# A graph-attention kernel whose adjacency mask is stored in another fp8 format and turned into its second form on another engine

## Chip, cores and metric

The kernel runs on one core of one Trainium2 chip. The metric is the device time in microseconds (us) of one execution. Where the text speaks of the profile, it is one profiled execution on that core: PE is the matrix engine (TensorE), PEld its weight loads, DVE the vector engine (VectorE), ACT the activation engine (ScalarE), POOL the general engine (GpSimd), SP the queue that issues most DMAs.

## What is computed

Two layers of masked multi-head attention over 16 images of 1024 nodes with 256 features, each behind a layer norm and a ReLU, with a residual. The layers differ in the number of heads (4 and 8), in the biases, and in the test on the adjacency: layer 0 keeps an edge where it is above 0, layer 1 where it is not 0.

```python
# layer 0
h = jnp.maximum(_layernorm(x, axis=-1), 0.0)
Q, K, V = ...                        # 4 heads of 64
scores = jnp.einsum('bhne,bhme->bhnm', Q, K) * scale
mask = adjacency_matrices[:, None, :, :] > 0
scores = jnp.where(mask, scores, -jnp.inf)
attn = jax.nn.softmax(scores, axis=-1)
x = x + heads(attn @ V) @ Wo.T + bo
# layer 1
h = jnp.maximum(_layernorm(x, axis=-1), 0.0)
q, k, v = ...                        # 8 heads of 32, with biases
scores = jnp.einsum('bhnd,bhmd->bhnm', q, k) / math.sqrt(D)
mask = adjacency[:, None, :, :] == 0
scores = jnp.where(mask, -jnp.inf, scores)
w = jax.nn.softmax(scores, axis=-1)
x = x + heads(w @ v) @ Wo.T + bo
```

The adjacency of the inputs holds zeros and ones. The kernel computes for any 32-bit integers: a fast program runs first, without subtracting the maximum of the scores; if a sum of exponentials left the range from 1e-15 to 1e15, a second, careful program does everything again (`verdict` and the `tc.If` at the end decide; it doesn't run with these inputs).

## The kernel before

**Stages and steps.** The fast program is one stream of steps. A stage is one layer of one image; the order is layer 0 of image 0, then for each image b layer 0 of image b+1 followed by layer 1 of image b, and at the end layer 1 of image 15. A layer-0 stage has 16 steps, a layer-1 stage 32. A step works on four blocks of 128 keys by 512 queries. `scores` (L400) makes them in two PSUM pairs, in layer 1 with four heads side by side in 32 rows of the array, in layer 0 with two in 64 rows. `exponentials` takes each pair through one VectorE instruction (L416: mask times BIG, minimum with the score, so that a masked score becomes hugely negative) and one exponential on ScalarE (L421). `weigh` (L433) multiplies by the values two steps later (LEAD = 2). The sums of exponentials come from additions of tiles, on VectorE and GpSimd in layer 0 (`add_tiles`, L442 to L448), on GpSimd (L534) and by accumulating DMAs (L520) in layer 1, and then from a matmul with a column block of ones (`count`, L301), are copied out (L320), spread by DMA (L333) and inverted (L341).

**Work around the stream.** Everything else is put by hand at numbered steps with `later(i, f, ...)` and is issued in step i after its exponentials. In one step, what has a place in `LARGE` or is a `turn` comes last (`rank`), so a `second` always comes ahead of a `turn`, `k`, `q`, `values` or `end_half` of the same step; otherwise the order is that of registration. An even step with such a large piece puts off its `weigh` to the next step. The pieces: `stats` and `norm` of the next inputs (L173, L174, GpSimd's L177 to L183, L190 on ScalarE), `turn` (transposes L208, copied by L209 on ScalarE), `k` and `q` (L225, copied by L231 to L239), `values` (L262, copied by L266), `end_half` (L381, added by L386). All of these and the scores share one PSUM pool of three pairs (`ps_s`, bufs=3), handed out in program order. A group's output (L433) is copied out of PSUM by L312 on ScalarE, between the two exponentials of a step, before the next group may weigh.

**The mask.** GpSimd issues the load of a tile of the adjacency as bf16 (L128), SP a DMA transpose (L134), and `put` (L143, ScalarE) writes adjacency - 0.5 in fp8 (float8e4) into one of five buffers of 8 x 512 bytes per partition. With BIG = 1e20 that is what layer 0 needs: above 0 is positive, all else negative. After layer 0 of the image has used it, `second` (L151, VectorE) rewrites two key blocks of a buffer at a time in place, to +0.5 where the adjacency is not 0 and -0.5 where it is. There are eight `second` per image. For images 0 to 14 they stand in the first 14 steps of layer 0 of the next image (steps a, a+2, a+4, a+6, a+8, a+10, a+12, a+13 with a that stage's first step). Image 15 has no next image: its eight stand in layer 1 of image 14, at steps c+8, c+10, ... c+22 with c that stage's first step.

**The test of the sums.** `test` (L247, VectorE) compares the spread sums of one layer of one image with the two bounds and multiplies the result into `chk`, 32 columns at a time: two instructions in layer 0 (32 columns of sums), four in layer 1 (64 columns). `chk` has 32 columns; `verdict` takes its minimum over columns (L742) and adds over partitions by a matmul (L744).

Of the kernel before, what the change touches and what calls it, by code (L numbers as in the profile page):

```python
# [10 lines left out]
F32 = mybir.dt.float32  # L11
BF16 = mybir.dt.bfloat16
I32 = mybir.dt.int32
F8 = mybir.dt.float8e4
AF = mybir.ActivationFunctionType
ALU = mybir.AluOpType
PSUM = bass.MemoryType.PSUM

P = 128
# [8 lines left out]

SUM_MIN, SUM_MAX = 1e-15, 1e15

BIG = 1e20

# [8 lines left out]
def load_weights(nc, const, a):  # L43

    w, loads = Weights(), []

    def mat(src, name):
        t = const.tile([P, 2, 256], F32, tag=name, name=name)
        loads.append((t, src.rearrange("(c p) f -> p c f", p=P)))
        return t  # L50

    def row(src, name):
        t = const.tile([P, 256], F32, tag=name, name=name)
        loads.append((t, src.partition_broadcast(P)))
        return t

    def col(src, name):
        t = const.tile([P, 2], F32, tag=name, name=name)
        loads.append((t, src.rearrange("(c p) -> p c", p=P)))
        return t  # L60

    w.k, w.q, w.v, w.o = [], [], [], []

    def mats(layer):
        for kind, of in (("k", w.k), ("q", w.q), ("v", w.v), ("o", w.o)):
            of.append(mat(a[f"w{kind}{layer}"], f"w{kind}{layer}"))

    mats(0)
    w.bo = [row(a["bo0"], "bo0"), row(a["bo1"], "bo1")]
    w.bq = col(a["bq1"], "bq1")  # L70
    w.bk = col(a["bk1"], "bk1")
    w.bv = col(a["bv1"], "bv1")
    mats(1)
    w.ident = const.tile([P, P], F32, tag="ident", name="ident")
    make_identity(nc, w.ident)
    w.ones = const.tile([P, 64], F32, tag="ones", name="ones")
    nc.gpsimd.memset(w.ones, 1.0)
    w.mhalf = const.tile([P, 4], F32, tag="mhalf", name="mhalf")
    nc.gpsimd.memset(w.mhalf, -0.5)
    return w, loads  # L80


def fast_program(ctx, tc, a, w, loads, chk):
# [3 lines left out]
    nc = tc.nc  # L87
    x, adj, out = a["x"], a["adj"], a["out"]
# [30 lines left out]
    class Mask:  # L119
# [16 lines left out]
        def put(self, t):  # L136

            qh = t // 4
            if t % 4 == 0:
                self.m[qh] = actp.tile(  # L140
                    [P, NT, 512], F8, tag="mask", bufs=5, name=f"mask_{self.b}_{qh}"
                )
            nc.scalar.activation(  # L143
                self.m[qh][:, :, ts(t % 4, P)], self.flipped.pop(t), AF.Identity,
                bias=w.mhalf[:, 0:1], saturate=False,
            )

        def second(self, u):

            m = self.m[u // 4][:, ts(u % 4, 2), :]  # L150
            nc.vector.tensor_scalar(  # L151
                m, m, -0.5, 0.5, op0=ALU.not_equal, op1=ALU.subtract, saturate=False
            )


    class Inputs:
# [85 lines left out]

        def test(self):

            for k in range(self.sums.shape[1] // 32):
                for bound, op in ((SUM_MIN, ALU.is_ge), (SUM_MAX, ALU.is_le)):
                    nc.vector.scalar_tensor_tensor(  # L247
                        out=chk, in0=self.sums[:, ts(k, 32)], scalar=bound, in1=chk,
                        op0=op, op1=ALU.mult,
                    )  # L250

        def k(self, half):
            self.kq(half, False)
# [18 lines left out]
    class Group:  # L272
# [23 lines left out]
        def count(self, p, start, stop):  # L296

            if start:
                self.s = ps_o.tile([P, 512], F32, tag="pz", name=f"pz_{self.n}")
            for r in range(self.per):  # L300
                nc.tensor.matmul(  # L301
                    self.s[r * self.D : (r + 1) * self.D, :], w.ones[:, : self.D], p[:, r, :],
                    start=start, stop=stop,
                )

# [11 lines left out]
        def spread(self):  # L317

            s = work.tile([P, 512], F32, tag="s", bufs=1, name=f"s_{self.n}")
            nc.scalar.copy(s, self.s)  # L320
            inp, k = self.inp, 2 * self.qh + self.g
            if k == 0:

                pool, tag = small, f"sums{self.layer}"
                if self.layer and inp.b == B - 1:
                    pool, tag = adjp, "adj"
                inp.sums = pool.tile(
                    [P, 4 * self.n_f], F32, tag=tag, bufs=1, name=f"sums_{inp.n}"
                )
            self.sn = inp.sums[:, k * self.n_f : (k + 1) * self.n_f]  # L330
            lanes = P // self.per
            for r in range(self.per):
                nc.sync.dma_start(  # L333
                    self.sn[r * lanes : (r + 1) * lanes, :],
                    s[r * self.D : r * self.D + 1, :].rearrange("r (c f) -> r c f", f=self.n_f),
                )
# [70 lines left out]
    def exponentials(st, between):  # L407


        gr = st.gr  # L410
        odd = st.j % 2
        st.p = pp.tile([P, 4, 512], F32, tag=f"p{odd}", bufs=2 if odd else 7, name=f"p_{st.n}")
        for i in range(2):
            half = st.p[:, ts(i, 2), :]
            kt = st.blocks[2 * i][1]
            nc.vector.scalar_tensor_tensor(  # L416
                out=half,
                in0=gr.mask.m[gr.qh][:, kt, :].unsqueeze(1).to_broadcast([P, 2, 512]),
                scalar=BIG, in1=st.ps[i], op0=ALU.mult, op1=ALU.min,
            )  # L420
            nc.scalar.activation(half, half, AF.Exp, scale=gr.scale)  # L421
            if i == 0:
                for f in between:
                    f()
# [34 lines left out]
    class Stream:  # L459
# [19 lines left out]
        def run(self):  # L479
# [3 lines left out]
            for i in range(n + LEAD):  # L483
# [21 lines left out]
                if now:  # L505
                    exponentials(now, copies)
                else:
                    for f in copies:
                        f()
# [80 lines left out]
    mask, inp = masks[0], inputs[0][0]  # L590
# [91 lines left out]
    for t in range(NT):  # L682
        i = 5 + 2 * t
# [52 lines left out]
def verdict(ctx, tc, w, chk):  # L736

    nc = tc.nc
    work = ctx.enter_context(tc.tile_pool(name="vwork", bufs=1))
    ps = ctx.enter_context(tc.tile_pool(name="vps", bufs=1, space=PSUM))  # L740
    row = work.tile([P, 1], F32, tag="row", name="row")
    nc.vector.tensor_reduce(row, chk, mybir.AxisListType.X, ALU.min)  # L742
    tot = ps.tile([1, 1], F32, tag="tot", name="tot")
    nc.tensor.matmul(tot, row, w.ones[:, 0:1], start=True, stop=True)  # L744
    bad = work.tile([1, 1], I32, tag="bad", name="bad")
    nc.vector.tensor_scalar(bad, tot, -1.0, float(P), op0=ALU.mult, op1=ALU.add)
    return bad
# [142 lines left out]
@with_exitstack  # L890
def kernel(
    ctx: ExitStack,
    tc: tile.TileContext,
    x: bass.AP,
    adj: bass.AP,
    wq0: bass.AP,
    wk0: bass.AP,
    wv0: bass.AP,
    wo0: bass.AP,
    bo0: bass.AP,  # L900
    wq1: bass.AP,
    bq1: bass.AP,
    wk1: bass.AP,
    bk1: bass.AP,
    wv1: bass.AP,
    bv1: bass.AP,
    wo1: bass.AP,
    bo1: bass.AP,
    out: bass.AP,
):  # L910
    nc = tc.nc
    a = dict(
        x=x, adj=adj, wq0=wq0, wk0=wk0, wv0=wv0, wo0=wo0, bo0=bo0, wq1=wq1, bq1=bq1,
        wk1=wk1, bk1=bk1, wv1=wv1, bv1=bv1, wo1=wo1, bo1=bo1, out=out,
    )
    B = x.shape[0]
    const = ctx.enter_context(tc.tile_pool(name="const", bufs=1))
    w, loads = load_weights(nc, const, a)
    chk = const.tile([P, 32], F32, tag="chk", name="chk")
    with ExitStack() as fast, tc.manual_schedule():  # L920
        fast_program(fast, tc, a, w, loads, chk)
    bad = verdict(ctx, tc, w, chk)
    flag = nc.values_load(bad[0:1, 0:1], min_val=0, max_val=P)
    with tc.If(flag > 0):
        with ExitStack() as careful:
            careful_program(careful, tc, a, w)
# [56 lines left out]
```

## Time and profile before

| what | us |
|---|---|
| runs: 3333.37, 3335.87, 3335.38; median | 3335.38 |
| profiled execution: span from first to last instruction | 3332.6 |
| a layer-0 stage (from 539.69 to 620.27) | 80.58 |
| a layer-1 stage (from 2867.10 to 2991.30) | 124.20 |
| layer 1 of images 14 and 15, to the end (from 3071.50) | 261.10 |
| `second` (L151): busy in all, mean of 128 | 178.6, 1.395 |
| `put` (L143): busy in all with a transposed tile, mean of 124 | 140.6, 1.135 |
| `test` (L247): busy in all, mean of 96 | 62.1, 0.647 |

The time of the profiled execution is not listed apart from its span; the runs lie 0.8 to 3.3 us above that span. The mean granted clock of TensorE is 0.993 of full speed. In a line of groups the numbers after the bar are the busy time and the mean duration in ns, and after the second bar the idle time of the engine just before. In a line of stretches each engine has its busy time with the number of instructions in brackets, then come the granted clock (1.00 is full speed), the share of the DMA engines and GB/s. In a line of the timeline come start, duration, engine, source line, operation and operands, and in square brackets the idle time of the engine just before it with what ended it. A stretch is given by its ends in us from the start of the span.

### The profile page before, as it was taken

The page shows a single profiled execution, that of the slowest core. Times are in us where ns is not written, and L with a number is a line of the kernel's source. Part 1 is how long each engine was busy: PE and PEld are TensorE (multiplying, and loading weights), DVE is VectorE, ACT ScalarE, POOL GpSimd, SP SyncE. Part 2 cuts the span into 40 slices and gives each one's busy share as a digit, 9 for nine tenths or more (in the row PEclk, how much of TensorE's full clock was granted, in tenths as well). Part 3 has the DMA queues.
Part 4 walks back from the last instruction along what each step waited for, and adds up shares of the span by engine and source line. Part 5 has one row for each costly group of instructions (what it writes and reads, how often), then busy time and mean ns, then how long its engine had stood idle before and what let it go on. Part 6 is the DMA issues. An engine that isn't in the chain of part 4 may idle for free.

```text
span 3332.6 us, 44087 instructions
## 1 busy us (share of the span) xinstructions
PE 3245.0 (97%) x16766; PEld 1272.4 (38%) x16766; DVE 2557.2 (77%) x2760; ACT 2178.2 (65%) x2402; POOL 2387.3 (72%) x1272
## 2 busy tenths in 40 slices
PE   8999999999999999999999999999999999999898
PEld 3443343433433333333434333343343343333333
DVE  5777877878778787786878768787787877878867
ACT  5567576675766757567575666757667576675565
POOL 4568586786867868677686776868778586785766
PEclk9999999999999999999999999999999999999999
DMA  7338467383664846548375573855738467482431
GB/s 145 63 67 148 97 111 140 73 153 86 121 128 82 157 83 131 113 93 149 77 141 102 105 138 77 146 103 112 138 74 152 96 112 139 80 149 52 89 77 31
DMA packets 313484, 361.08 MB, mean 108 GB/s; under 512 B 190000, under 2 KB 257840, under 8 KB 290480
## 3 DMA queue, kind: packets, MB, share of 16 engines
q0 software_dynamic: 77856, 253.78, 42.1%
q1 hardware_dynamic: 235408, 104.41, 14.0%
q8 instruction: 133, 2.18, 0.3%
q14 instruction: 87, 0.71, 0.1%
HBM read 119.54 MB, written 17.56 MB: 41 GB/s over the span
## 4 chain that ended last, share of the span: by engine, by line
PE 73%; POOL 8%; DMA 7%; DVE 5%; issue 3%; ACT 3%; SPq 1%; POOLq 0%; DVEq 0%; ACTq 0%
PE ps L400 24%; PE po L433 21%; PE pq L225 11%; PE pv L262 7%; PE py L381 5%; POOL p L534 5%; DMA p<-p 4%; DVE p L416 4%; PE pz L301 3%; DMA adjT<-adj 2%; ACT p L421 1%; PE ph L208 1%; POOL p L445 1%; ACT mask L143 1%; DVE p L442 1%
## 5 line engine op out<-in xcount | busy, mean ns | idle before, releaser
L416 DVE SCALAR_TENSOR_TENSOR p<-mask,ps 128x1024 f32<-128x1024 fp8e4 x1536 | 1790.7, 1213 | 598.6 <-PE ps L400 509.9
L421 ACT ACTIVATE p<-p 128x1024 f32<-128x1024 f32 x1536 | 1616.8, 1057 | 960.6 <-DVE p L416 915.2
L534 POOL TENSOR_TENSOR p<-p,p 128x2048 f32<-128x2048 f32 x255 | 1201.7, 4714 | 181.5 <-PE po L433 162.2
L400 PE MATMUL ps<-qT,kT 32*128 32x512 f32 (+1 forms) x6144 | 1196.0, 635 | 37.4 <-DVE p L416 35.6
L433 PE MATMUL po<-p,v 128*32 128x512 f32 (+1 forms) x6144 | 994.0, 603 | 1.0 <-ACT cat L312 0.9
L400 PEld LDWEIGHTS ps<-qT,kT 32*128 32x128 f32 (+1 forms) x6144 | 382.4, 185 | 739.5 <-issue 358.6
L446 POOL TENSOR_TENSOR p<-p 128x1024 f32<-128x1024 f32 x128 | 319.7, 2497 | 273.4 <-DVE p L445 268.4
L433 PEld LDWEIGHTS po<-p,v 128*32 128x32 f32 (+1 forms) x6144 | 229.1, 118 | 691.7 <-issue 503.6
L445 POOL TENSOR_TENSOR p<-p 128x1024 f32<-128x1024 f32 x64 | 151.4, 2366 | 236.2 <-DVE p L442 151.8
L262 PE MATMUL pv<-wv,hT 128*128 128x256 f32 x1024 | 239.5, 387 | 14.6 <-ACT hT L209 14.5
L520 POOL DMA_DIRECT2D p<-p x178 | 178.8, 1005 | 98.1 <-DMA p<-p 66.1
L225 PE MATMUL pq<-hT,wk 128*128 128x512 f32 x512 | 239.6, 611 | 2.8 <-ACT hT L209 2.8
L225 PE MATMUL pq<-hT,wq 128*128 128x512 f32 x512 | 240.0, 612 | 0.1
L381 PE MATMUL py<-wo,cat 128*128 128x256 f32 x1008 | 235.8, 387 | 3.3 <-ACT hT L209 1.0
L262 PEld LDWEIGHTS pv<-wv,hT 128*128 128x128 f32 x1024 | 190.6, 191 | 88.1 <-ACT hT L209 26.8
L381 PEld LDWEIGHTS py<-wo,cat 128*128 128x128 f32 x1008 | 188.3, 191 | 74.7 <-issue 46.3
L352 POOL TENSOR_TENSOR cat<-cat,inv 128x512 f32<-128x512 f32 x127 | 178.8, 1408 | 7.5 <-DMA inv<-vd 6.3
L151 DVE TENSOR_SCALAR mask<-mask 128x1024 fp8e4<-128x1024 fp8e4 x128 | 178.6, 1395 | 0.0
L442 DVE TENSOR_TENSOR p<-p 128x1024 f32<-128x1024 f32 x128 | 161.4, 1261 | 0.0
L448 POOL TENSOR_TENSOR p<-p,p 128x1024 f32<-128x1024 f32 x64 | 152.4, 2381 | 5.0
L301 PE MATMUL pz<-p,ones 128*32 128x512 f32 (+1 forms) x888 | 148.7, 595 | 4.6 <-DMA p<-p 3.8
L225 PEld LDWEIGHTS pq<-hT,wk 128*128 128x128 f32 x512 | 93.2, 192 | 145.1 <-issue 103.5
(50 smaller groups left out, 1696.0 us busy)
## 6 DMA issues: line engine op xcount, KB each, us to landing
p<-p POOLq DMA_DIRECT2D x178, 1024.0 KB, 8.8
adj<-in_adj_dram POOLq DMA_DIRECT2D x128, 256.0 KB, 4.4
x<-bo POOLq DMA_DIRECT2D x64, 512.0 KB, 6.0
x<-in_x_dram SPq DMA_DIRECT2D x32, 512.0 KB, 4.1
inv<-vd SPq DMA_DIRECT2D x128, 128.0 KB, 2.9
inv<-vd SPq DMA_DIRECT2D x252, 64.0 KB, 2.9
out_dram<-x SPq DMA_DIRECT2D x31, 512.0 KB, 3.1
sums<-s SPq DMA_DIRECT2D x384, 2.0 KB, 3.4
```

What stands on the lines that cost most here:

```text
L225: nc.tensor.matmul(pq[:, m, :], wt[self.layer][:, c, ts(m, P)], self.hT[half][:, c, :], start=(c == 0), stop=(c == 1),)
L262: nc.tensor.matmul(pv[:, i, :], self.hT[half][:, c, ts(i, P)], w.v[self.layer][:, c, :], start=(c == 0), stop=(c == 1),)
L301: nc.tensor.matmul(self.s[r * self.D : (r + 1) * self.D, :], w.ones[:, : self.D], p[:, r, :], start=start, stop=stop,)
L381: nc.tensor.matmul(py[:, i, :], self.half.cat[:, c, ts(i, P)], w.o[self.layer][:, c, :], start=(c == 0), stop=(c == 1),)
L400: nc.tensor.matmul(st.ps[i // 2][:, i % 2, :], gr.inp.kT[r * D : (r + 1) * D, gr.g, ts(kt, P)], gr.inp.qT[gr.qh][r * D : (r + 1) * D, gr.g ...
L416: nc.vector.scalar_tensor_tensor(out=half, in0=gr.mask.m[gr.qh][:, kt, :].unsqueeze(1).to_broadcast([P, 2, 512]), scalar=BIG, in1=st.ps[i] ...
L421: nc.scalar.activation(half, half, AF.Exp, scale=gr.scale)
L433: nc.tensor.matmul(gr.o[r * D : (r + 1) * D, :], gr.inp.v[:, kt, h * D : (h + 1) * D], st.p[:, i, :], start=(kt == 0), stop=(kt == NT - 1),)
L442: nc.vector.tensor_add(a, a, b)
L445: engine.tensor_add(b, two.p[:, 0:2, :], two.p[:, 2:4, :])
L446: nc.gpsimd.tensor_add(a, a, b)
L534: nc.gpsimd.tensor_add(one, one, st.p)
```

## The change

The mask is kept in float8e5, a format with a wider exponent. `put` now writes 2 x 8192 x adjacency - 8192, that is 8192 or -8192 for the adjacency of these inputs; layer 0 still multiplies by BIG, now 1e15. `second` becomes one activation on ScalarE: the absolute value of the first form plus 8192, that is 0 where the adjacency is 0 and 16384 where it is 1. In layer 1, L416 adds -8192 to that and takes the minimum with the score, so a masked score becomes -8192, whose exponential is 0. The places of `put` and `second` in the order of steps stay as they are.

The test takes all columns of the sums at once, two instructions in either layer, and `chk` has 64 columns for it. The block of ones shrinks to one column that `count` broadcasts, and the biases of the two activations stand in one small tile with the -0.5 that the norm uses.

```diff
-F8 = mybir.dt.float8e4
+F8 = mybir.dt.float8e5
...
-BIG = 1e20
+BIG = 1e15
+EDGE = 8192.0
...
-    w.ones = const.tile([P, 64], F32, tag="ones", name="ones")
+    w.ones = const.tile([P, 1], F32, tag="ones", name="ones")
     nc.gpsimd.memset(w.ones, 1.0)
-    w.mhalf = const.tile([P, 4], F32, tag="mhalf", name="mhalf")
-    nc.gpsimd.memset(w.mhalf, -0.5)
+    numbers = const.tile([P, 6], F32, tag="numbers", name="numbers")
+    w.mhalf, w.below, w.above = numbers[:, 0:4], numbers[:, 4:5], numbers[:, 5:6]
+    for of, value in ((w.mhalf, -0.5), (w.below, -EDGE), (w.above, EDGE)):
+        nc.gpsimd.memset(of, value)
...
             nc.scalar.activation(
                 self.m[qh][:, :, ts(t % 4, P)], self.flipped.pop(t), AF.Identity,
-                bias=w.mhalf[:, 0:1], saturate=False,
+                bias=w.below, scale=2.0 * EDGE, saturate=False,
             )
...
             m = self.m[u // 4][:, ts(u % 4, 2), :]
-            nc.vector.tensor_scalar(
-                m, m, -0.5, 0.5, op0=ALU.not_equal, op1=ALU.subtract, saturate=False
-            )
+            nc.scalar.activation(m, m, AF.Abs, bias=w.above, saturate=False)
...
-            for k in range(self.sums.shape[1] // 32):
-                for bound, op in ((SUM_MIN, ALU.is_ge), (SUM_MAX, ALU.is_le)):
-                    nc.vector.scalar_tensor_tensor(
-                        out=chk, in0=self.sums[:, ts(k, 32)], scalar=bound, in1=chk,
-                        op0=op, op1=ALU.mult,
-                    )
+            part = chk[:, : self.sums.shape[1]]
+            for bound, op in ((SUM_MIN, ALU.is_ge), (SUM_MAX, ALU.is_le)):
+                nc.vector.scalar_tensor_tensor(
+                    out=part, in0=self.sums, scalar=bound, in1=part, op0=op, op1=ALU.mult,
+                )
...
-                    self.s[r * self.D : (r + 1) * self.D, :], w.ones[:, : self.D], p[:, r, :],
+                    self.s[r * self.D : (r + 1) * self.D, :], w.ones.to_broadcast([P, self.D]), p[:, r, :],
...
-            self.sn = inp.sums[:, k * self.n_f : (k + 1) * self.n_f]
+            self.sn = inp.sums[:, ts(k, self.n_f)]
...
-                scalar=BIG, in1=st.ps[i], op0=ALU.mult, op1=ALU.min,
+                scalar=-EDGE if gr.layer else BIG, in1=st.ps[i],
+                op0=ALU.add if gr.layer else ALU.mult, op1=ALU.min,
...
-    chk = const.tile([P, 32], F32, tag="chk", name="chk")
+    chk = const.tile([P, 64], F32, tag="chk", name="chk")
```

## The prediction

> **What bounds the kernel now.** I read the busy shares first, then the groups by line for the operations that the diff touches, then the busy time of each engine in stretches cut at the stage borders (a stage is one layer of one image; the border is where the score matmuls at L400 change from 64-row to 32-row form), and last the timeline where TensorE stood still.
>
> ```profile
> PE 3245.0 (97%) x16766; PEld 1272.4 (38%) x16766; DVE 2557.2 (77%) x2760; ACT 2178.2 (65%) x2402; POOL 2387.3 (72%) x1272
> ...
> L151 DVE TENSOR_SCALAR mask<-mask 128x1024 fp8e4<-128x1024 fp8e4 x128 | 178.6, 1395 | 0.0
> ```
>
> TensorE is busy for 97%, so 87 us at most are idle; VectorE's 178.6 us in L151 are not for the taking by themselves. The question is where those 128 instructions stand.
>
> ```profile
> core 0: us, PE busy (x) PEld busy (x) DVE busy (x) ACT busy (x) POOL busy (x), PEclk, DMA share, GB/s
> ...
> 539.69:620.27 80.58, 80.24 (x345) 31.24 (x344) 67.90 (x71) 43.81 (x49) 48.44 (x27) 1.00 0.45 99
> ...
> 2867.10:2991.30 124.20, 121.64 (x698) 47.89 (x696) 91.32 (x102) 92.19 (x103) 102.03 (x55) 0.99 0.69 124
> 3071.50:3332.60 261.10, 233.22 (x1444) 87.25 (x1442) 195.12 (x194) 156.66 (x167) 178.04 (x65) 0.95 0.30 64
> ...
> 539.69:620.27 80.58, 10.58 (x8) 1.00 0.45 99
> ...
> 2867.10:2991.30 124.20, 0.00 (x0) 0.99 0.69 124
> 3071.50:3332.60 261.10, 21.01 (x8) 0.95 0.30 64
> ```
>
> The first rows are all engines, the last three L151 alone. A layer-0 stage (539.69) holds 8 of the second forms, 10.6 us of VectorE, but TensorE is idle there for 80.58 - 80.24 = 0.34 us: all of L151 is hidden. A layer-1 stage (2867.10) holds none. The last stretch, layer 1 of images 14 and 15, holds 8 that take 21.0 us, and TensorE is idle for 27.9 us. That is the only place where L151 can be on the path. Here is the worst spot of it, in order of time:
>
> ```profile
> 3114.98 8.43 DVE L151 TENSOR_SCALAR mask<-mask 128x1024 fp8e4<-128x1024 fp8e4 x1
> ...
> 3116.34 1.09 PE L208 MATMUL ph<-ident,hn 128*128 128x128 f32 x8
> 3116.71 1.61 POOL L198 DMA_DIRECT2D x<-bo  x1
> 3117.55 5.29 POOL L534 TENSOR_TENSOR p<-p,p 128x2048 f32<-128x2048 f32 x1
> 3121.99 1.70 POOL L520 DMA_DIRECT2D p<-p  x1
> 3123.32 2.34 DVE L416 SCALAR_TENSOR_TENSOR p<-mask,ps 128x1024 f32<-128x1024 fp8e4 x2
> ...
> 3124.59 1.22 PE L400 MATMUL ps<-qT,kT 32*128 32x512 f32 x2 [7.15 <-DVE p L416]
> ```
>
> One L151 lasts 8.43 us instead of its minimum of 0.66 (GpSimd works all the while); L416 and, 7.15 us later, TensorE wait for it. The same happens at 3156.35: an L151 of 6.26 us, TensorE idle for 5.29. And after both, the clock drops:
>
> ```profile
> 3124.60:3127.80 3.20, 3.20 (x9) 1.02 (x9) 2.15 (x2) 2.98 (x3) 0.00 (x0) 0.50 1.01 205
> 3127.80:3131.00 3.20, 3.20 (x8) 2.57 (x9) 1.86 (x3) 2.11 (x2) 0.00 (x0) 0.50 0.41 82
> ...
> 3163.80:3166.90 3.10, 3.10 (x8) 1.00 (x8) 2.05 (x2) 2.99 (x3) 0.00 (x0) 0.50 1.04 211
> ```
>
> The granted clock is 0.50 there, against 1.00 elsewhere: L381's 16 matmuls take 6.14 us instead of 3.72, L262's 16 take 5.37 instead of 3.72.
>
> **What the Trainium skill says.** (1) "GPSIMD Engine Reference", Key points: GpSimd shares its SBUF interfaces with VectorE, with contention for VectorE instructions in a two-port mode or with two SBUF inputs. The trace agrees: L151 runs from 0.66 to 8.43 us, and the long ones lie beside GpSimd's work. (2) "TensorE: Matmul & The Clock Gate", What's actually happening: an idle window of about 3.4 us halves the clock. The trace agrees: 0.50 after gaps of 7.15 and 5.29 us. (3) "ScalarE: Activation LUTs", Table sets: abs, relu and identity are in every set, so beside exp they need no table load; the trace shows one load (1283 ns) for relu, identity, copy and exp together, and no Abs. (4) The same page, Rules for kernel authors: about 0.3 us plus 0.83 ns per element, an estimate of 1.15 us for 1024 elements.
>
> **The change part by part.**
>
> *Abs on ScalarE in place of L151.* No row shows an activation that reads fp8. The nearest is L143 (bf16 in, fp8 out, bias a column): 1135 ns. From below a copy of that size takes 1003 ns (L209); a bound from above is twice L143, 2.27 us, if fp8 were read at half speed. I take 1.13 us. It can't gain below nothing on its own engine.
>
> In layer-0 stages ScalarE goes from 43.8 to 43.8 + 8 x 1.13 = 52.9 us of 80.6. What waits behind an Abs is the next step's exponentials (L421), and for these the weighing (L433) two steps later. At 1595.67 the scores of a step start, its exponentials end at 1600.29, its weighing is due at 1605.16 at the earliest: 4.9 us of slack against 1.13. Cost and gain: 0, TensorE being the bound. The 14 layer-0 stages that follow could give at most 0.34 us each.
>
> *The last stretch.* Call its first step c (3071.5). The forms come at c+8, c+10, ... c+22. At c+10: without L151, L416 of step c+11 can start when its scores end (3114.27 + 1.14 = 3115.4) instead of 3123.32, and TensorE has its buffers for the scores of c+12 by 3118. Next late is ScalarE. The PSUM pool has 3 pairs, taken in the order scores, scores, ph (L208), scores, scores, py (L381): L381 needs the pair that L209 empties on ScalarE, and L209 queues behind the exponentials and now two Abs. From 3110.26, the end of c+8's exponentials: two hn 1.0, Abs 1.13, exp 1.06, cat 0.5, exp 1.06, two hn 1.0, two exp 2.2, Abs 1.13, two exp 2.2, hT 1.0: 12.3 us, so 3122.5. L381 starts then, after an idle gap of some 3.2 us, and at full clock ends at 3122.5 + 3.72 = 3126.2 instead of 3133.94. **Gain 7.7 us.**
> At c+18: ScalarE is free at 3157.97; Abs 1.13, two exp 2.2, hT 1.0: 3162.3. L262 starts then (before: 3166.93), takes 3.72 instead of 5.37 and ends at 3166.0 instead of 3172.3. **Gain 6.3 us**, with a gap of some 2.6 us left.
> At c+22: L400 at 3179.67 takes 2.31 us behind L151; the one before it, where no form stands between, 1.51. **Gain 0.8 us.**
> c+8: 1.45 us leave VectorE, but the Abs makes the cat copy (L312), on which the weighing waits, some 0.7 us later; already in the chain above, 0. c+12, c+14, c+16 and c+20 lie beside matmul groups of 3.7 us: 0. If that cover were gone, their L151 would give 0.69 + 0.66 + 1.78 + 0.69 = 3.8 us.
>
> *L416 with add for mult, fp8 with a wider exponent.* Same shape, bytes and operand sources: 0. The trace has no other fp8 kind; a change of 1% of L416's 1213 ns would be hidden in layer 0 and could be some us either way in the layer-1 stages.
>
> *Sums checked at once.* 96 instructions become 64. All but the last ten lie in layer-0 stages (4.12 us each), hidden. The last ten (L247 at 3323.06, 2.2 us) become six, about 0.8 us less, but the reduction behind them (L742, 3325.59) waits for the output's DMA anyway: 0. Its 64 columns instead of 32 cost 0.03 us.
>
> *Ones broadcast, memsets.* Weight loads from a broadcast column (L645) take 188 ns, from a matrix 190 (L381): 0. Two memsets more at the start, 0.1 us each, before a GpSimd gap of 6.0 us: 0.
>
> **Sum:** 7.7 + 6.3 + 0.8 = 14.8 us. The profiled span is 3332.6; the runs are 0.8 to 3.3 us above it, and their median 2.8, which I take for what lies around it. 3332.6 - 14.8 = 3317.8, and with 2.8 us **3320.6**.
>
> **Rivals.**
> A. *No ScalarE bill.* If L209 came early enough, L381 could end at about 3122.3 (11.5 us gained) and L262 at 3163.4 (8.9), with c+8 and c+22 giving 2: 22 us, 3313. For it speaks ScalarE's 7.5 us of idle time in the stall; against it the queue order worked out above. Chance 0.15.
> B. *The clock stays low.* The gap of 3.2 us that is left is near the 3.4 us of the page. Then L381 and L262 keep 6.14 and 5.37: 14.8 - 2.4 - 1.7 = 10.7, 3324.7. An Abs of 2.27 us, three of which lie in the two chains, gives the same (14.8 - 3 x 1.14 = 11.4). Chance 0.15.
> C. *Hardly any change,* within 6.7 us: another engine holds the last stretch (GpSimd works 49 of the 76 us from 3105.6 to 3182, and its additions at L534 free the buffers), or the layer-1 stages, which last 122.6 to 125.6 us for equal work, fall out otherwise by some 5 us in sum. Some 3331. Chance 0.13.
> D. *Slower: Abs is not in the loaded table set.* Then every Abs brings two switches at the page's 2.66 us (load and drain): 1.13 + 5.3 = 6.4 us. In a layer-0 stage ScalarE would need 43.8 + 51 = 95 us against 80.6: 14.4 us for each of the 14 later stages, some 200 us, and some 18 in the last stretch, where it would need 43.4 + 51 of 76.4: about 3550. It decides from (80.6 - 43.8) / 8 = 4.6 us for one form on; 1.13 is far below. Against it speaks the skill and the single load in the trace. With the smaller chance that L416 itself is slower: 0.07.
> My own case has 0.50.
>
> **The numbers.** A measurement here can tell about 0.2%, 6.7 us, from no change. Faster: 0.50 + 0.15 + 0.15 = 0.80; within: 0.13; slower: 0.07. The range takes in A and B with their bounds, 8 to 23 us gained: 3312.5 to 3327.5.
>
> **What would show it.** In the changed profile: layer-0 stages still 80.6 us with ScalarE near 53 and VectorE near 57; L151's row as an activation on ACT of 1.0 to 1.2 us; no more than one table load; no L416 preceded by a VectorE operation of over 3 us in the last stretch; the last stretch some 15 us shorter; the matmuls at L381 and L262 there at 3.7 us, each waiting for ACT hT (L209) first. Wrong: stages that were unbroken before and get TensorE gaps on ACT p (L421), or a clock of 0.5 still in the last stretch.

## The result, and the profile after

Twenty runs of the changed kernel have a median of 3329.52 us (3322.25 to 3337.90); twenty of the kernel before, 3340.63 us (3333.37 to 3356.33). The ratio is 0.9964, with a 95% interval of 0.9953 to 0.9976: 8 to 16 us faster. The forecast was 3320.6 us with a range of 3312.5 to 3327.5, so the measured time lies 2 us outside it. As a ratio to the three runs that it started from, the forecast was 3320.6 / 3335.38 = 0.9956, which the interval holds; the level it started from was low by 5 us, and one step of the sum was wrong besides. Either alone would have left the time within the range (3320.6 + 5.3 or + 3.7 us). Both are taken apart below.

The page of the changed kernel: shares of the engines, then two groups by line (busy time, mean ns). Some line numbers are one higher here than in the kernel before: the transposes are L209, their copies L210, the accumulating DMA L521 and GpSimd's long addition L535; the names of the tiles stay the same.

```profile
PE 3245.4 (97%) x16766; PEld 1272.1 (38%) x16766; DVE 2391.8 (72%) x2600; ACT 2308.4 (69%) x2530; POOL 2349.9 (70%) x1274
...
L416 DVE SCALAR_TENSOR_TENSOR p<-mask,ps 128x1024 f32<-128x1024 fp8e5 x1536 | 1793.8, 1215 | 698.8 <-PE ps L400 606.5
...
L154 ACT ACTIVATE mask<-mask,numbers 128x1024 fp8e5<-128x1024 fp8e5 x128 | 145.0, 1133 | 0.0
```

The second form is now L154 on ScalarE, 1133 ns (forecast 1.13 us), and L416 with the addition and the other format takes 1215 ns against 1213 before. There is still one table load. This profiled execution has a span of 3335.1 us, longer than the 3332.6 of the one before, although the runs say the opposite. The stretches show why (all engines; an inner layer-0 stage, a layer-1 stage, the last stretch):

```profile
538.98:619.88 80.90, 79.93 (x346) 31.32 (x345) 58.30 (x61) 52.02 (x57) 45.77 (x27) 1.00 0.46 98
2883.27:3007.35 124.08, 120.69 (x699) 47.43 (x697) 90.98 (x102) 92.20 (x103) 101.87 (x54) 1.00 0.68 124
3088.36:3335.13 246.77, 227.94 (x1444) 84.79 (x1442) 174.74 (x182) 163.72 (x175) 177.88 (x65) 0.97 0.31 68
```

The last stretch is down from 261.1 to 246.8 us. ScalarE in a layer-0 stage is at 52.0 us and VectorE at 58.3, within some 1 us of the forecast (near 53 and near 57). But the layer-0 stage grew (80.58 to 80.90 here; the median of the 14 later ones went from 80.58 to 80.99): TensorE is now idle in it for 80.90 - 79.93 = 1.0 us where it was 0.34. And one layer-1 stage of this execution lasted 132.07 us where its neighbour took 124.78; the chain of waits names its cause in one step, an accumulating DMA:

```profile
1848.85:1980.92 132.07, 127.12 (x699) 49.05 (x697) 90.99 (x102) 92.32 (x103) 101.89 (x54) 0.95 0.73 119
1643.16:1767.94 124.78, 121.97 (x698) 48.06 (x696) 90.88 (x102) 92.18 (x103) 101.85 (x54) 0.99 0.69 123
```

```profile
1941.72 15.86 DMA p<-p
```

In the execution before, no DMA of this kind (L520) took longer than 11.93 us. So single executions differ by 7 us and more through one such DMA, and stages have to be compared with stages.

**The last stretch, c+10 to c+12.** The same place as in the prediction, 3088.36 - 3071.50 = 16.86 us later (all engines, in order of time):

```profile
3134.29 1.13 ACT L154 ACTIVATE mask<-mask,numbers 128x1024 fp8e5<-128x1024 fp8e5 x1
3134.40 5.33 POOL L535 TENSOR_TENSOR p<-p,p 128x2048 f32<-128x2048 f32 x1
3135.25 1.09 PE L209 MATMUL ph<-ident,hn 128*128 128x128 f32 x8
3135.33 1.99 ACT L422 ACTIVATE p<-p 128x1024 f32<-128x1024 f32 x2
3136.27 1.14 PE L400 MATMUL ps<-qT,kT 32*128 32x512 f32 x8
3137.22 0.99 ACT L210 COPY hT<-ph 128x1024 f32<-128x1024 f32 x1
...
3138.36 3.69 PE L381 MATMUL py<-wo,cat 128*128 128x256 f32 x16 [0.94 <-ACT hT L210]
```

GpSimd's long addition (L535) still stands there, but VectorE no longer waits for it: the scores of c+12 follow the transposes at once, L381 takes 3.69 us instead of 6.14, and what it waits for is ScalarE's copy L210, 0.94 us. The stretch from the end of c+8's exponentials to L381 shows ScalarE without a break, and inside it the clock, low for a while (all engines):

```profile
3127.03:3138.21 11.18, 9.04 (x52) 2.62 (x48) 7.57 (x7) 11.18 (x15) 11.07 (x5) 0.85 0.77 151
3131.50:3134.90 3.40, 3.40 (x20) 0.72 (x16) 1.07 (x1) 3.40 (x6) 3.40 (x4) 0.50 0.58 118
```

**The layer-0 stage.** The place where TensorE waits, before and then after (L520 and L521 are the same accumulating DMA, the second of two in the stage):

```profile
1586.74 1.48 DVE L151 TENSOR_SCALAR mask<-mask 128x1024 fp8e4<-128x1024 fp8e4 x1
1587.61 0.87 POOL L520 DMA_DIRECT2D p<-p  x1
1588.14 0.24 DVE L341 RECIPROCAL vn<-sums 128x16 f32<-128x16 f32 x1
1588.41 0.36 SPq L343 DMA_DIRECT2D vd<-vn  x1
...
1594.67 1.06 PE L301 MATMUL pz<-p,ones 128*32 128x512 f32 x8 [0.24 <-DMA p<-p]
1594.91 1.70 SPq L346 DMA_DIRECT2D inv<-vd  x4
```

```profile
1586.85 0.25 DVE L341 RECIPROCAL vn<-sums 128x16 f32<-128x16 f32 x1
1587.12 0.36 SPq L343 DMA_DIRECT2D vd<-vn  x1
1587.71 0.86 POOL L521 DMA_DIRECT2D p<-p  x1
...
1588.64 3.34 SPq L346 DMA_DIRECT2D inv<-vd  x4
...
1595.60 1.06 PE L301 MATMUL pz<-p,ones 128*32 128x512 f32 x8 [1.05 <-DMA p<-p]
```

Before, L151 held the reciprocal L341 until the accumulating DMA had been issued. The small write behind the reciprocal (L343) was issued 0.8 us after that DMA, and the four broadcasts that need it (L346) left only when the DMA was over. After, the reciprocal runs 1.4 us sooner (measured from that DMA's issue), the write is ahead of the accumulating DMA, and the broadcasts are issued 0.9 us behind that DMA's issue. It lands in 7.84 us instead of 7.02 (median of the 14 stages), and the matmul with the ones, TensorE's next work, waits for it.

### The profile page after: what moved, and what is told of

Read it like the earlier page. It is cut to its first block, busy times and chain, and to the rows that moved or that the text cites. A ratio compares the mean times of both kernels' runs of the same rounds, so it can differ in the third digit from the quotient of the medians.

```text
span 3335.1 us, 44057 instructions
## 1 busy us (share of the span) xinstructions
PE 3245.4 (97%) x16766; PEld 1272.1 (38%) x16766; DVE 2391.8 (72%) x2600; ACT 2308.4 (69%) x2530; POOL 2349.9 (70%) x1274
## 4 chain that ended last, share of the span: by engine, by line
PE 72%; POOL 8%; DMA 8%; DVE 4%; ACT 4%; issue 3%; SPq 1%; POOLq 0%; DVEq 0%; ACTq 0%
PE ps L400 24%; PE po L434 21%; PE pq L226 11%; PE pv L262 6%; POOL p L535 5%; PE py L381 5%; DMA p<-p 4%; PE pz L301 3%; DVE p L416 3%; DMA adjT<-adj 2%; ACT p L422 2%; PE ph L209 1%; POOL p L446 1%; ACT mask L146 1%; DMA vd<-vn 1%
## 5 line engine op out<-in xcount | busy, mean ns | idle before, releaser
L416 DVE SCALAR_TENSOR_TENSOR p<-mask,ps 128x1024 f32<-128x1024 fp8e5 x1536 | 1793.8, 1215 | 698.8 <-PE ps L400 606.5
L535 POOL TENSOR_TENSOR p<-p,p 128x2048 f32<-128x2048 f32 x255 | 1202.5, 4718 | 171.0 <-PE po L434 157.7
L447 POOL TENSOR_TENSOR p<-p 128x1024 f32<-128x1024 f32 x128 | 301.8, 2358 | 298.3 <-DVE p L446 293.2
L446 POOL TENSOR_TENSOR p<-p 128x1024 f32<-128x1024 f32 x64 | 151.5, 2367 | 253.8 <-DVE p L443 169.4
L262 PE MATMUL pv<-wv,hT 128*128 128x256 f32 x1024 | 237.8, 385 | 16.2 <-ACT hT L210 16.2
L521 POOL DMA_DIRECT2D p<-p x178 | 178.5, 1003 | 95.1 <-DMA p<-p 66.6
L381 PE MATMUL py<-wo,cat 128*128 128x256 f32 x1008 | 233.9, 385 | 3.1 <-ACT hT L210 1.9
L262 PEld LDWEIGHTS pv<-wv,hT 128*128 128x128 f32 x1024 | 189.4, 190 | 88.5 <-ACT hT L210 27.7
L381 PEld LDWEIGHTS py<-wo,cat 128*128 128x128 f32 x1008 | 186.5, 190 | 72.8 <-issue 46.4
L301 PE MATMUL pz<-p,ones 128*32 128x512 f32 (+1 forms) x888 | 148.7, 595 | 16.2 <-DMA p<-p 15.4
L312 ACT COPY cat<-po 128x512 f32<-128x512 f32 x128 | 74.0, 578 | 115.9 <-PE po L434 115.9
L226 PEld LDWEIGHTS pq<-hT,wq 128*128 128x128 f32 x512 | 94.3, 194 | 146.2 <-issue 119.9
```

The lines of the kernel that those rows point to most:

```text
L226: nc.tensor.matmul(pq[:, m, :], wt[self.layer][:, c, ts(m, P)], self.hT[half][:, c, :], start=(c == 0), stop=(c == 1),)
L262: nc.tensor.matmul(pv[:, i, :], self.hT[half][:, c, ts(i, P)], w.v[self.layer][:, c, :], start=(c == 0), stop=(c == 1),)
L301: nc.tensor.matmul(self.s[r * self.D : (r + 1) * self.D, :], w.ones.to_broadcast([P, self.D]), p[:, r, :], start=start, stop=stop,)
L381: nc.tensor.matmul(py[:, i, :], self.half.cat[:, c, ts(i, P)], w.o[self.layer][:, c, :], start=(c == 0), stop=(c == 1),)
L416: nc.vector.scalar_tensor_tensor(out=half, in0=gr.mask.m[gr.qh][:, kt, :].unsqueeze(1).to_broadcast([P, 2, 512]), scalar=-EDGE if gr.layer ...
L446: engine.tensor_add(b, two.p[:, 0:2, :], two.p[:, 2:4, :])
```

## The experiments

My theory after the result had two parts: (1) all that is won lies in the last stretch; (2) in each layer-0 stage two DMAs changed their order, which costs TensorE some of it. The rivals were that ScalarE's Abs, or the format, makes the layer-0 loss, and that VectorE's own time, not its wait for GpSimd, made the stalls. Stage lengths from the profile of each run, in us (layer-0: median of the 14 later ones; layer-1: sum of the 13 after the first), with the ratio to the kernel before:

| run | layer-0 | last stretch | layer-1 | ratio, interval |
|---|---|---|---|---|
| before | 80.58 | 261.1 | 1609 | |
| changed | 80.99 | 246.8 | 1621 | 0.9964, 0.9953 to 0.9976 |
| e1_last_on_act | 80.18 | 245.4 | 1614 | 0.9944, 0.9921 to 0.9967 |
| e2_rest_on_act | 80.97 | 261.6 | 1620 | 1.0007, 0.9990 to 1.0024 |
| e3_none_on_act | 80.17 | 261.4 | 1615 | 0.9990, 0.9976 to 1.0003 |
| e4_invert_later | 80.18 | 245.9 | 1634 | 0.9950, 0.9930 to 0.9970 |
| e5_before_form_later | 81.37 | 262.5 | 1610 | 1.0040, 1.0026 to 1.0054 |
| e6_twice_on_act | 80.97 | 253.9 | 1613 | 0.9989, 0.9979 to 0.9998 |
| e7_last_left_out | 80.97 | 246.2 | 1621 | 0.9963, 0.9951 to 0.9976 |
| e8_act_and_dve | 80.98 | 259.3 | 1611 | 1.0007, 0.9990 to 1.0024 |
| e9_both_moved | 80.18 | 245.2 | 1626 | 0.9946, 0.9926 to 0.9966 |
| e10_act_and_dve_again | 80.98 | 248.0 | 1611 | 0.9969, 0.9955 to 0.9982 |
| e11_before_test | 80.17 | 260.1 | 1623 | 0.9988, 0.9975 to 1.0000 |
| e12_before_last_moved | 80.59 | 255.4 | 1622 | 0.9987, 0.9974 to 0.9999 |

**e1: ScalarE for image 15 alone.**

```diff
-            nc.scalar.activation(m, m, AF.Abs, bias=w.above, saturate=False)
+            if self.b < x.shape[0] - 1:
+                nc.vector.tensor_scalar(
+                    m, m, -EDGE, 2.0 * EDGE, op0=ALU.not_equal, op1=ALU.mult, saturate=False
+                )
+            else:
+                nc.scalar.activation(m, m, AF.Abs, bias=w.above, saturate=False)
```

> The changed kernel, but only the eight second forms of image 15 (those in the last stretch) are made on ScalarE; those of images 0 to 14 go back to VectorE as one tensor_scalar on the new format (not equal to -8192, times 16384). My theory: all that is won lies in the last stretch, and the layer-0 stages only lose, because without the form ahead of it the reciprocal L341 starts 1.4 us sooner and its write is issued ahead of the accumulating DMA. So here: layer-0 stage back at 80.6 us, last stretch near 246.8, in all some 14 us below before (ratio about 0.9957). Rival (the loss in the layer-0 stages is due to the format or the addition in L416): layer-0 stage stays at 81.0.

Measured: 80.18 and 245.4 us, ratio 0.9944. With 120 of the 128 forms back on VectorE the kernel keeps the whole gain of the last stretch, so in the later stages the other 120 win nothing by leaving VectorE. The layer-0 stage is shorter than expected, below that of the kernel before; e3 and e11 say why.

**e2: all others on ScalarE, image 15 on VectorE** (the same edit with the condition turned round).

> The changed kernel, but the eight second forms of image 15 go back to VectorE, the other 120 stay on ScalarE. My theory: nothing is won and the layer-0 stages lose 0.4 us each: layer-0 stage 81.0 us, last stretch near 261 with TensorE gaps of 5 to 7 us and a clock of 0.5 behind them, in all 5 to 6 us above before (ratio about 1.0017). Rival (120 forms taken off VectorE are worth something in the layer-1 stages that follow them): below before by several us with the last stretch still at 261.

Measured: 80.97 and 261.6 us, ratio 1.0007, whose interval holds the expected 1.0017. No sign of a gain in the layer-1 stages. With e1 this settles part (1) but for one place that the theory overlooked: the first two layer-0 stages, taken together, last 168.5 us in the kernel before, in e1 and in e3, and 167.6 to 167.7 in the changed kernel and in e2. There the forms on ScalarE win some 0.8 us; why was not followed up.

**e3: no form on ScalarE** (all 128 as in e1's first branch).

> The changed kernel with all 128 second forms back on VectorE (one tensor_scalar on the new format, not equal to -8192, times 16384). What stays of the change is the format, the addition in L416, the test of all columns at once and the broadcast ones. My theory: of these only the test does anything: two instructions less on VectorE per layer-1 test take away a delay of 0.4 us in each layer-0 stage. So layer-0 stage 80.2 us, layer-1 stages as before (near 123.8), last stretch near 261 with its two long VectorE stalls: some 5 us below before (ratio about 0.9985). Rival (format and addition matter): the layer-1 stages, where L416 adds, change by over 0.5 us each, or L416's mean moves off 1213 ns.

Measured: layer-0 stage 80.17, last stretch 261.4, L416's mean 1212 ns. The format, the addition and the broadcast ones do nothing that shows; 0.4 us per layer-0 stage come off without any form leaving VectorE. The ratio, 0.9990, fits the expected 0.9985 and doesn't exclude 1.

**e4: the inversion one step later**, in the changed kernel.

```diff
-                at = (8, 12, 17, 19) if gr.qh == 0 else (8, 11, 14)
+                at = (8, 12, 17, 19) if gr.qh == 0 else (8, 12, 14)
```

> The changed kernel with the inversion of the sums of one group per layer-1 stage (third of four, the one whose L341 falls in step 4 of the next layer-0 stage) put one step later, so that its write is issued behind the accumulating DMA again. My theory (two DMAs changed their order): that DMA lands in 7.0 us instead of 7.8, the matmul with the ones (L301) waits 0.2 us instead of 1.05, layer-0 stage 80.6 us, some 5 us below the changed kernel. Rival (ScalarE's Abs makes the loss): layer-0 stage stays at 81.0, the DMA still at 7.8.

Measured: the DMA lands in 7.03 us and the layer-0 stage falls to 80.18, below the 80.6 that was expected (e3 and e11 say why), with ScalarE's 51.9 us in it unchanged. The ratio, 0.9950, goes the right way, but its interval overlaps that of the changed kernel. In order of time, the same place:

```profile
1595.23 0.85 POOL L521 DMA_DIRECT2D p<-p  x1
1595.43 1.13 ACT L154 ACTIVATE mask<-mask,numbers 128x1024 fp8e5<-128x1024 fp8e5 x1
...
1602.28 1.07 PE L301 MATMUL pz<-p,ones 128*32 128x512 f32 x8 [0.24 <-DMA p<-p]
1602.48 0.25 DVE L341 RECIPROCAL vn<-sums 128x16 f32<-128x16 f32 x1
```

The Abs stands beside the DMA as before, the reciprocal now comes after it, and L301 waits 0.24 us. The rival, ScalarE, falls.

**e5: the order of the DMAs changed in the kernel before**, by moving one form of each image.

```diff
-        for i, u in zip((0, 2, 4, 6, 8, 10, 12, 13), range(NT)):
+        for i, u in zip((0, 2, 5, 6, 8, 10, 12, 13), range(NT)):
```

> The kernel before with one second form per image (the third, step 4 of the layer-0 stage) put one step later, so that L341 of step 4 no longer stands behind it. No ScalarE, no new format. My theory: the write is issued ahead of the accumulating DMA here too, which then lands in 7.8 us; layer-0 stage 81.0 us, in all some 5 us above before (ratio about 1.0016), last stretch 261. Rival (ScalarE or the format): layer-0 stage 80.6, ratio 1.000.

Measured: ratio 1.0040 (1.0026 to 1.0054), layer-0 stage 81.37 us, the DMA 7.81 us. The direction is as expected and the size twice that: 0.8 us per stage, because the 0.4 us that the changed kernel saves elsewhere in the stage are not saved here.

```profile
1588.87 0.25 DVE L341 RECIPROCAL vn<-sums 128x16 f32<-128x16 f32 x1
1589.15 0.36 SPq L343 DMA_DIRECT2D vd<-vn  x1
1589.75 0.86 POOL L520 DMA_DIRECT2D p<-p  x1
1590.67 3.33 SPq L346 DMA_DIRECT2D inv<-vd  x4
...
1597.63 1.06 PE L301 MATMUL pz<-p,ones 128*32 128x512 f32 x8 [1.06 <-DMA p<-p]
```

The old format, no Abs, and the same wait of 1.06 us: part (2) is shown from both sides. The two runs show what the order costs; whether it is the small write ahead of the DMA or the broadcasts beside it that lengthen it, they don't separate.

**e6: ScalarE's bill doubled.**

```diff
             nc.scalar.activation(m, m, AF.Abs, bias=w.above, saturate=False)
+            nc.scalar.activation(m, m, AF.Identity, saturate=False)
```

> The changed kernel with a second activation (Identity, in place, without a bias) behind every Abs: it doubles ScalarE's bill and leaves the result as it is. My theory (ScalarE costs nothing in the layer-0 stages, but is on the path in the last stretch): layer-0 stage stays at 81.0 us, the accumulating DMA at 7.8; last stretch 3 to 4 us longer than 246.8, since three of these activations lie in the two chains that end in the copies L210. Rival (the layer-0 loss comes from ScalarE): layer-0 stage goes to 81.4 or more.

Measured: layer-0 stage unchanged at 80.97, so eight more activations cost nothing there. The last stretch is 7.1 us longer, not 3 to 4:

```profile
3160.20 1.14 ACT L154 ACTIVATE mask<-mask,numbers 128x1024 fp8e5<-128x1024 fp8e5 x1
3161.38 1.06 ACT L155 ACTIVATE mask<-mask 128x1024 fp8e5<-128x1024 fp8e5 x1
3162.34 1.99 ACT L423 ACTIVATE p<-p 128x1024 f32<-128x1024 f32 x2
3164.23 0.99 ACT L211 COPY hT<-ph 128x1024 f32<-128x1024 f32 x1
...
3165.27 6.47 PE L263 MATMUL pv<-wv,hT 128*128 128x256 f32 x16 [2.97 <-ACT hT L211]
```

Both activations stand ahead of the copy that frees the PSUM pair. TensorE waits 2.97 us for it, and the 16 matmuls behind take 6.47 us instead of 3.72: the clock was 0.50 from 3165.2 to 3169. Of the 7.1 us the cooled clock makes 2.75 here; the rest, 4.3, has another low stretch of the clock in it (3123.1 to 3126.5) and is not far from what was reckoned for the waits.

**e7: image 15 without a second form.** In layer 1 of image 15, L416 multiplies the first form by BIG; the eight `second` are dropped.

```diff
-                scalar=-EDGE if gr.layer else BIG, in1=st.ps[i],
-                op0=ALU.add if gr.layer else ALU.mult, op1=ALU.min,
+                scalar=-EDGE if gr.layer and gr.inp.b < B - 1 else BIG, in1=st.ps[i],
+                op0=ALU.add if gr.layer and gr.inp.b < B - 1 else ALU.mult, op1=ALU.min,
...
-            for u in range(NT):
-                later(c + 8 + 2 * u, masks[b + 1].second, u)
```

> The changed kernel, where image 15 has no second form at all: its layer 1 uses the first form with the multiplication by BIG, as layer 0 does (right for adjacencies of 0 and 1, so the test on negative values is left out for this image). It shows what ScalarE's eight Abs cost in the last stretch. By the prediction's sums: 22 us won with no Abs against 14.8 with them, so last stretch near 239 to 240. Rival (ScalarE has room in the stretch, and another wait ends last): within 2 us of 246.8. Layer-0 stages 81.0 in either case.

Measured: 246.2 us, within 1 us of the changed kernel: the rival is right. Measured from the stretch's start, the scores of step c+25 begin 95.9 us in, against 97.9 in the changed kernel and 114.1 before; so the eight Abs cost 2 us there, and by c+36 (127.2 against 128.1) half of that is gone again. TensorE still waits 0.95 and 0.86 us for the copies L210 with no Abs in front of them. (The stretch's total hides some of this, since its last matmuls differ between executions; see below.)

**e8: VectorE's time put back, without the wait for GpSimd.**

```diff
             nc.scalar.activation(m, m, AF.Abs, bias=w.above, saturate=False)
+            if self.b == x.shape[0] - 1:
+                for k in range(3):
+                    waste = small.tile(...)
+                    nc.vector.bn_stats(waste, xs[self.b, 0][:, k, :])
```

> The changed kernel, with Abs on ScalarE, and beside each of the eight second forms of image 15 three bn_stats on VectorE into a tile that nobody reads (0.42 us each, 1.3 us in all, nearly twice what L151 took at its fastest; this instruction kept its 0.42 us beside GpSimd everywhere in the kernel before). It puts VectorE's time back without the wait for GpSimd. My theory (the stalls of 8.4 and 6.3 us are waits for GpSimd, and these cooled the clock): last stretch within 5 us of 246.8, no TensorE gap over 3 us, clock 1.00 there. Rival (VectorE's own time in these places makes the stall): last stretch back above 255.

Measured: 259.3 us, with a TensorE gap of 7.12 us. It tells nothing: one of these instructions waited 7.6 us for the DMA x<-bo that adds the bias to the rows it reads. e10 reads a weight tile instead (`w.v[0][:, 0, :]`).

> The run with three bn_stats beside each Abs of image 15 again, now reading a constant weight tile: the one before read the rows of x, and its third instruction waited 7.6 us for the DMA that adds the bias to them, so it told nothing. Work for VectorE of 1.3 us per form, in the places where L151 stood, but without a wait for GpSimd. My theory: last stretch within 5 us of 246.8, no TensorE gap over 3 us and no clock of 0.5 behind one. Rival (VectorE's own time in these places makes the stall): last stretch above 255.

Measured: 248.0 us. Some 1.3 us of VectorE's time in each of the eight places cost 1.3 us by the end of the stretch, and 2.7 us by the scores of its last step (222.6 us from its start against 220.0). Part of this is a clock of 0.50 from 3131.5 to 3134.8, while L381 runs behind a gap of 1.86 us, so that detail of the expectation fails. VectorE's time alone doesn't make the stalls; the wait for GpSimd does.

**e9: the inversion later, and Abs at other steps.** e4's edit, and

```diff
-            for u in range(NT):
-                later(c + 8 + 2 * u, masks[b + 1].second, u)
+            for u, i in enumerate((12, 13, 14, 16, 20, 21, 22, 24)):
+                later(c + i, masks[b + 1].second, u)
```

> The changed kernel with the one inversion per layer-1 stage a step later (as in the run that moved it alone) and with the eight Abs of image 15 at steps c+12, 13, 14, 16, 20, 21, 22 and 24 instead of every second step from c+8, so that none stands ahead of the copies L312 and L210 that TensorE waited for. My theory: layer-0 stage 80.2 us, last stretch 245 to 246 (the run with no Abs at all for image 15 gave 246.2 with its last py matmuls 1.4 us longer than in other runs), in all some 17 to 19 us below before (ratio about 0.9945), 5 to 6 below the changed kernel. Rival (what is saved at these steps is waited for elsewhere, or the accumulating DMA is late for another reason): no better than the changed kernel, ratio 0.9964.

Measured: 80.18 and 245.2 us as expected, ratio 0.9946 (0.9926 to 0.9966). By the stages it beats the changed kernel by 14 x 0.8 + 1.6 = 13 us; the ratios differ by 6 us and their intervals overlap, so the whole time doesn't show it beyond doubt. Most of it is e4's one digit.

**e11: the test alone, in the kernel before** (with the column of ones).

> The kernel before with the test of all columns at once and the broadcast column of ones (which makes room for the wider chk), nothing else: second forms, format and L416 as before. My theory: the two instructions less per layer-1 test end VectorE's work 0.4 us sooner, L151 six steps later in the layer-0 stage waits that much less for GpSimd, and the scores there no longer wait: layer-0 stage 80.2 us instead of 80.6, the rest as before, ratio about 0.9983. Rival (the 0.4 us come from the new format or the addition): layer-0 stage stays at 80.6.

Measured: layer-0 stage 80.17, ratio 0.9988 (0.9975 to 1.0000). Two instructions less in the layer-1 test shorten L151 six steps later (2.46 us instead of 2.87, since GpSimd's addition starts and ends 0.42 us sooner), and the scores behind it take 1.99 us instead of 2.26. The changed kernel saves these 0.4 us too; it has no L151 there. Of the 0.41 us, 0.31 come off TensorE's busy time (80.24 to 79.93) and only 0.10 off its idle time: a wait can hide in matmuls that the profile counts as busy. The last stretch, 260.1, is 1 us shorter than before; its last DMA and end were not followed up.

**e12: the forms of image 15 moved, still on VectorE** (e9's second edit in the kernel before).

> The kernel before with the eight second forms of image 15, still on VectorE, at steps c+12, 13, 14, 16, 20, 21, 22 and 24 instead of every second step from c+8. My theory (an L151 is long where GpSimd works without a pause, at c+10 and c+18, and short at steps where GpSimd waits): no L151 over 3 us, no TensorE gap over 3 us, last stretch about 247, so the same 14 us as the change brings, without ScalarE (ratio about 0.9957). Rival (wherever it stands, L151 is held by GpSimd for some us): long ones turn up at the new places and the last stretch stays above 255.

Measured: 255.4 us; neither theory. The long waits at the old places are gone, but others turn up. In order of time:

```profile
3173.39 4.53 POOL L534 TENSOR_TENSOR p<-p,p 128x2048 f32<-128x2048 f32 x1 [5.80 <-issue]
...
3174.61 3.86 DVE L151 TENSOR_SCALAR mask<-mask 128x1024 fp8e4<-128x1024 fp8e4 x1
...
3179.76 2.08 PE L400 MATMUL ps<-qT,kT 32*128 32x512 f32 x4 [2.58 <-DVE p L416]
```

L151 comes 1.2 us into a GpSimd addition and ends 0.55 us after it (3178.47 against 3177.92). Moving it makes the wait shorter, not sure to be short. What follows costs more than the wait of 2.58 us itself: for 10.2 us, nearly all of them busy, TensorE has half its clock, by estimate some 5 us more than at full clock:

```profile
3179.60:3189.80 10.20, 10.04 (x23) 2.89 (x24) 9.73 (x8) 6.33 (x6) 4.90 (x2) 0.50 0.84 172
```

Taking the forms off VectorE gave 14 us, moving them 6.

## Why the prediction was right or wrong

**Right: the last stretch.** Forecast -14.8 us, measured 246.77 - 261.11 = -14.3; e1 got -15.7 (the last stretch alone). Term by term, from the stretch's start: L381 ends 8.7 us sooner (forecast 7.7), the pv matmuls (L262) a further 7.1 (forecast 6.3), the scores of c+25 a further 0.4 (forecast 0.8), which makes 16.2. Of these 0.4 us are given back by the last step and 1.5 us behind it, where the output matmuls L367 take 7.2 us from first to last instead of 5.9; with the same code there e1 and e4 have 5.9 and 6.2, e7 and e9 7.3 and 7.5, so this varies between executions. The clock behind the two old stalls was rightly counted: about 4 us of the gain.

**Right in kind, too large: ScalarE's bill.** The chain that was summed does bind: from 3127.03 to 3138.21 ScalarE works without a break, through the same instructions in the same order, and L381 starts behind its last copy. It takes 11.1 us and not 12.3, and L381 starts 1.0 us sooner than forecast. The sum used durations, while activations that follow each other at once start 0.1 us before the one ahead has ended (two exponentials in 1.99 us, not 2.12). The wait of 3.2 us came in two pieces, 1.33 us for the copy L312, which the first Abs delays, and 0.94 us for L210. The second is small because the clock was low just before it: in e1, where it stayed at 1.00, TensorE waits 1.98 us there and L381 starts at the same 50.0 us from the stretch's start. At L262 the wait is 1.65 us (forecast 2.6). Rival A, 22 us without that bill, falls with e7: with no Abs at all, L381 starts only 1.2 us sooner, and 1 us is left at the end.

**Wrong: "Cost and gain: 0, TensorE being the bound", said of the layer-0 stages.** TensorE's 0.34 us of idle time per stage was read as if it bounded both what could be won and what could be lost. It bounds neither: e11 won 0.41, most of it from time counted as busy, and e5 lost 0.79. The prediction asked of ScalarE what waits behind the new instruction, but of VectorE only how much time goes, not what runs sooner. What ran sooner was a reciprocal whose write and broadcasts then met a 1 MB accumulating DMA: +0.8 us in each of 14 stages (e4, e5). The lines that show it were in the trace of before: L520 at 1587.61, L151 ending at 1588.22, L343 at 1588.41, and a wait of 0.24 us at L301 for exactly that DMA. Against it stands -0.4 us from VectorE's shorter work; the test of the sums gives it alone (e3, e11), where the prediction had "hidden". Net 0.405 x 14 = 5.7 us.

**Wrong: the level.** The three runs shown, 3333.4 to 3335.9, were near the lower end of what the kernel before does: in the runs that followed it took from 3330 to 3365 us. 5.3 of the 8.9 us by which 3320.6 was too low are that (3340.63 - 3335.38). The rest, 3.7 us, is the forecast change of 14.8 less the measured 11.1: the layer-0 stages put in 5.7, the last stretch 0.5, the first two layer-0 stages take out 0.8, and 1.7 stay untraced, within the scatter of the runs. Nor were the 2.8 us what lies around the span: every run on record with a span listed took 1.7 to 1.9 us more than its own span, so 1.0 us of them was the difference between executions. One source of the scatter is seen in the traces: in seven of the fourteen profiled executions, of old and new code alike, one or two layer-1 stages after the first last 130 to 136 us instead of some 124, and in these an accumulating DMA took 13.7 to 20.1 us; in the executions without such a stage none took over 13.6. What delays it stays open. Rival C named the layer-1 stages as a source of some 5 us; a single such stage costs more than that, and nothing shows that the change makes them.

**Rivals B and D.** In the changed kernel L381 runs at full speed behind the gap that is left. B's reason was sound all the same: the window of about 3.4 us that the Trainium skill gives ("TensorE: Matmul & The Clock Gate", What's actually happening) is no safe bound for a single gap. A gap of 2.97 us was enough for a clock of 0.50 in e6. In the changed kernel the clock was 0.50 from 3131.5 to 3134.9, after a gap of only 1.33 us that had ended 0.9 us before, while in e1 gaps of 1.35 and 1.98 us at the same places left it at 1.00. In the two profiled executions of the kernels before and after, each low stretch but those of the last 25 us lasts 3.41, 6.83 or 10.24 us, which fits such a window. It need not be idle throughout: in the 3.41 us ahead of 3131.5 TensorE was busy for 2.1. It was luck that the changed kernel's low stretch fell where TensorE waited for ScalarE anyway. D falls: Abs needed no table load beyond the one of before, as the same skill's page on ScalarE ("ScalarE: Activation LUTs", Table sets) has it.


## What to carry to other kernels

Where an engine is taken off work that is hidden, list what runs sooner and which DMAs that issues, and against which transfer they will now stand; a stage whose bound engine hardly idles can still lose. Look for the rare place where the same work is not hidden (here 8 of 128 instructions held nearly all of the gain) and price the cold clock behind a stall with it. And compare stages, not single executions, when one DMA can cost more than the edit.

## What the runs showed of the hardware

- In the kernel before, 84 of the 128 VectorE tensor_scalar (L151) start while GpSimd is at an instruction. In 83 of them L151 ends 0.55 to 0.60 us after the computation that GpSimd is at, or, where it is issuing a DMA, after the computation behind it; the other 44 take 0.7 us. The one exception is the longest: at 3114.98, 8.43 us, L151 comes near the end of an addition and is held on through a multiplication, a DMA issue and another addition, which it outlasts by 0.57 us. Why it was not let in after the first stays open. bn_stats in the same places (e10) kept its 0.42 us.
- An 8 KB write issued 0.8 us after a 1 MB accumulating DMA landed 6.4 us later; issued 0.6 us ahead of it, in 1.5 us. With that write ahead of it and four broadcasts issued beside it, the DMA lasted 7.8 us instead of 7.0.
- Activations from fp8 to fp8 (L154) take 1133 ns for 1024 elements, as from bf16 to fp8 (L143 of before, 1135 ns).
